# Latent attention in fp32 splits: staging of one group's rotary weights, and the queue of the output's first operands

## The chip, the cores and the metric

The kernel runs on one core of a Trainium2 chip. The metric is the device time of one execution in microseconds (us). Engines are named as in the profile: PE (TensorE), DVE (VectorE), ACT (ScalarE), POOL (GpSimd) and SP (SyncE, which only issues transfers here).

## The reference

One transformer layer on a sequence of S = 2048 rows of HID = 512: multi-head latent attention with 16 heads, residual and layer norm, then a linear layer with a scale and a bias, residual and layer norm.

```python
cq = rms_norm(x @ w_qa.T, q_a_ln_w)                  # 384 wide
q  = (cq @ w_qb.T)  -> 16 heads of 128 "nope" + 64 rotary
ckv = x @ w_kva.T                                    # 128 latent + 64 rotary
kv  = rms_norm(ckv[:, :128]) @ w_kvb.T               # k_nope 128, v 128 per head
scores = (q_nope . k_nope + rot(q_pe) . rot(k_pe)) * 192**-0.5   # causal
out = softmax(scores) @ v @ w_o.T
x = layernorm(x + out)
x = layernorm(x + (x @ (weight * scale_weight).T + bias))
```

## The kernel before

**The arithmetic.** Products in fp32 are made of two parts, a high one in the PE's fast fp32 format and the rest, so each product is three matmuls: high by high, high by low, low by high. The helper `split` makes both parts: ACT copies the high part (L64, or L67 with a scale) and DVE subtracts it (L65, L68). Keys are kept as latent rows: `Kn` (normalised latent, columns of keys) and `Kp` (rotary part), both for all 2048 keys, two parts each. Queries are brought into the latent space instead, by a weight product per head.

**Weights of the queries.** The heads come in four groups g of four. `weights_q(g)` prepares a group. For each of three slices `lt` it loads the rotary weights `rpe` (L159, on ACT's queue), splits them with the norm weight `qln` into a staging tile, and SP writes that to the DRAM tile `wpe_d[g]` (L169). Then for each slice it loads `wqb` (L174, ACT's queue), multiplies it on PE with `wk` (`ps_wq`, L179), splits the product into a staging tile and SP writes it to `wq_d[g]`. Both are loaded back when a pair of heads is projected: `wq` (`load_wq`, L352) and `wpe` (`load_wpe`, L358), by way of `move` (L59), on POOL's queue in block 0. Group 0 has a direct form: its split parts go to `wq0` and `wpe0` for the first use, and the second half of each product goes through staging tiles `wst` (L186).

**Staging.** `places` gives the staging tiles of groups 1 to 3. Keys beyond 1024 aren't used until later blocks, so 512-column pieces A to D of `Kn` and `Kp` (A and B are columns 1536 to 2047, C and D 1024 to 1535) serve as staging. Where `places` holds None, a tile of the ring with tag `st` is taken: three buffers, which `wst`, `cqst` (the compressed queries' staging) and group 1's `wpst` share. Raw loads share the tag `wraw`, with four buffers.

**Blocks and units.** The queries come in NB = 4 blocks of 512 rows, and in each block the heads come in eight pairs. Block 0 (128 to 512 keys) runs together with the projection of the rest of x and with the preparation of groups 1 to 3; there an automatic scheduler sets the order of the instructions on every engine. From block 1 on, PE and SP run in program order, and from the first pair's second quarter of block 3 ACT and DVE do as well (L729). POOL's place is always the scheduler's. In block 3 a unit is one head and one quarter of the rows, k = 0 to 7 in a pair:

- `head_scores`: PE makes the scores in two PSUM tiles (L438), DVE takes the maximum (L510), ACT the exponential into a tile `pr` (L532). Three PSUM tiles rotate, and the `pr` tiles have five buffers.
- `head_probs`: ACT makes a half-precision high part of `pr` (L563) and POOL the low part (L564), DVE transposes (L546), and SP writes the result into a `ring` in SBUF with four transfers (`turn`, L553). A `pr` tile is free again only when its ring transfers have landed.
- `values`: later, PE multiplies the ring's probabilities with V (L619). The result is scaled and goes to DRAM as `ot_d`.

**The output.** The output weights `wo` and the value weights `wv` are multiplied into `wvo` per pair (`value_output`, PE tile `ps_wo`, L198). `prepare_output(b, p, k)` runs ahead of each unit of the last block and loads what the output needs first: `wv` in pair 6 before unit 2, and in pair 7 `wo0` before unit 1, the attention results `o` with their inverse row sums `iv` of block 0, pair 0 and 1 (`latent_load`, L823, and `latent_rows`, L839), before units 2 and 3, and `wo1` before unit 4. `latent_split` uses `o` and `iv` before units 5 and 6 (L849). A third `o` is loaded before unit 7 on POOL's queue. `accumulate` (L888) adds the output's products.

```python
        if (p, k) == (NPAIR - 2, 2):
            state["wv"] = blk.tile([P, H, P], F32, tag="pe", name="wv")
            nc.gpsimd.dma_start(state["wv"], a["wv"])
```

## Time and profile before

| what | value |
|---|---|
| time, median of 3 runs | 1637.24 us (1637.19 to 1637.43) |
| the profiled execution: time, span | 1638.56 us, 1636.8 us |
| mean granted PE clock | 0.99 |
| busy share of the span: PE, DVE, ACT, POOL | 96%, 69%, 56%, 52% |
| longest ACT wait for a ring transfer; in all | 4.9 us; 61.1 us |
| PE idle for the exponential (L532) before scores | 13.9 us in 10 waits |

A line of the timeline has the start in us, the busy time in us, the engine, the source line, the operation with output and inputs, the shape and the count; in brackets stand the idle time of the engine ahead of it and what ended that. ACTq, POOLq and SPq are the same engines when they issue transfers. A window's line has the window, its length, and the busy time of PE, PE's weight loads, DVE, ACT and POOL with the number of instructions, then the mean granted PE clock, the mean busy share of the DMA engines and GB/s. The clock row shows the granted clock in tenths of full speed for 40 equal slices; 9 is 90% or more.

### The profile page before, as it was taken

The page shows a single profiled execution, that of the slowest core. Times are in us where ns is not written, and L with a number is a line of the kernel's source. Part 1 is how long each engine was busy: PE and PEld are TensorE (multiplying, and loading weights), DVE is VectorE, ACT ScalarE, POOL GpSimd, SP SyncE. Part 2 cuts the span into 40 slices and gives each one's busy share as a digit, 9 for nine tenths or more (in the row PEclk, how much of TensorE's full clock was granted, in tenths as well). Part 3 has the DMA queues.
Part 4 walks back from the last instruction along what each step waited for, and adds up shares of the span by engine and source line. Part 5 has one row for each costly group of instructions (what it writes and reads, how often), then busy time and mean ns, then how long its engine had stood idle before and what let it go on. Part 6 is the DMA issues. An engine that isn't in the chain of part 4 may idle for free. (4 is left out here: it accounts for less than half of the span.)

```text
span 1636.8 us, 27536 instructions
## 1 busy us (share of the span) xinstructions
PE 1575.2 (96%) x9292; PEld 1294.5 (79%) x9292; DVE 1130.0 (69%) x1874; ACT 918.3 (56%) x1529; POOL 846.0 (52%) x701
## 2 busy tenths in 40 slices
PE   9799998899999999999999999999999998999998
PEld 7688876788888888888887778888887776678876
DVE  5668665577677777777777678778677676575464
ACT  5557564666665757666665665666666654321120
POOL 2345553454554766667765566666666665011011
PEclk9899999999999999999999999999999999999999
DMA  6988676676776878787787767867777777962030
GB/s 213 265 238 267 194 203 164 175 185 172 191 206 171 217 179 202 162 206 181 199 195 180 177 153 174 184 160 160 177 156 192 211 178 210 320 197 77 32 117 33
DMA packets 259436, 297.60 MB, mean 182 GB/s; under 512 B 35264, under 2 KB 227136, under 8 KB 258272
## 3 DMA queue, kind: packets, MB, share of 16 engines
q1 hardware_dynamic: 241008, 251.63, 55.4%
q0 software_dynamic: 11376, 34.52, 12.0%
q10 hardware_dynamic: 6912, 9.70, 2.0%
q8 instruction: 74, 1.21, 0.3%
q14 instruction: 66, 0.54, 0.1%
HBM read 99.94 MB, written 36.44 MB: 83 GB/s over the span
## 5 line engine op out<-in xcount | busy, mean ns | idle before, releaser
L564 POOL TENSOR_TENSOR hlpr<-pr,hlpr 128x1024 f16<-128x1024 f32 (+3 forms) x320 | 613.2, 1935 | 327.2 <-ACT hlpr L563 297.9
L438 PE MATMUL s<-Kn,qn 128*128 128x512 f32 (+4 forms) x1920 | 510.3, 373 | 22.3 <-ACT pr L532 13.9
L532 ACT ACTIVATE pr<-s,bias,rq 128x1024 f32<-128x1024 f32 (+3 forms) x320 | 325.4, 1021 | 343.2 <-issue 178.3
L510 DVE TENSOR_REDUCE neg<-s 128x1 f32<-128x1024 f32 (+3 forms) x320 | 310.0, 985 | 133.2 <-PE s L441 75.0
L438 PEld LDWEIGHTS s<-Kn,qn 128*128 128x128 f32 x1920 | 334.3, 189 | 72.7 <-ACT pr L532 19.9
L619 PE MATMUL o<-ring,V 128*128 128x256 f16 x3024 | 373.1, 273 | 7.4 <-DMA ring<-pr 5.3
L546 DVE STREAM_TRANSPOSE pr<-hlpr 128x1024 f32<-128x1024 f32 (+7 forms) x256 | 311.5, 1223 | 97.9 <-POOL hlpr L564 72.2
L438 PE MATMUL s<-Kp,pe 128*128 128x512 f32 (+4 forms) x1280 | 362.9, 364 | 5.5 <-DMA pe<-prod 5.5
L619 PEld LDWEIGHTS <-V 128*128 128x128 f16 x3264 | 301.1, 96 | 82.7 <-issue 32.0
L563 ACT ACTIVATE hlpr<-pr 128x1024 f16<-128x1024 f32 (+3 forms) x320 | 338.2, 1113 | 4.9 <-DVE pr L546 1.0
L438 PEld LDWEIGHTS s<-Kp,pe 128*128 128x128 f32 x1280 | 233.6, 189 | 36.4 <-DMA pe<-prod 5.7
L410 PE MATMUL ps_qn<-cq,wq 128*128 128x512 f32 x576 | 150.0, 405 | 2.1 <-DMA wq<-wq_d 1.9
L989 POOL TENSOR_TENSOR lnr<-lnt,nhalf 128x1 f32<-128x1 f32 x32 | 21.3, 671 | 213.3 <-DVE lnt L988 213.2
L410 PEld LDWEIGHTS ps_qn<-cq,wq 128*128 128x128 f32 x576 | 105.5, 192 | 23.1 <-DVE xl L65 1.1
L68 DVE SCALAR_TENSOR_TENSOR qn<-ps_qn,kvln,qn 128x512 fp32r<-128x512 f32 x64 | 47.5, 744 | 45.5 <-ACT qn L67 45.2
L599 POOL TENSOR_TENSOR hl<-pr,hl 128x128 f16<-128x128 f32 (+3 forms) x64 | 56.8, 908 | 37.7 <-ACT hl L598 37.3
L372 PE MATMUL ps_pe<-cq,wpe 128*128 128x512 f32 x288 | 75.3, 407 | 0.2 <-DMA cq<-cq_d 0.2
L64 ACT ACTIVATE oh<-o 128x1024 fp32r<-128x1024 f32 x28 | 29.7, 1061 | 79.6 <-PE acc L888 49.1
L888 PE MATMUL acc<-wvo,oh 128*128 128x512 f32 x224 | 71.5, 401 | 1.0 <-ACT pr L532 0.6
L64 ACT ACTIVATE xt<-tp 128x512 fp32r<-128x512 f32 x16 | 9.6, 598 | 94.8 <-PE tp L1008 94.8
L532 ACT ACTIVATION_READ_ACCUMULATOR pr<-s,bias,rq 128x1 f32 x320 | 61.8, 193 | 0.0
L372 PEld LDWEIGHTS ps_pe<-cq,wpe 128*128 128x128 f32 x288 | 53.4, 193 | 10.6 <-issue 0.3
(458 smaller groups left out, 1777.4 us busy)
## 6 DMA issues: line engine op xcount, KB each, us to landing
ring<-pr SPq DMA_DIRECT2D x384, 128.0 KB, 2.9
wq<-wq_d SPq DMA_DIRECT2D x22, 768.0 KB, 6.7
ring<-pr SPq DMA_DIRECT2D x128, 112.0 KB, 3.4
o<-ot_d SPq DMA_DIRECT2D x28, 512.0 KB, 5.5
ot_d<-ot SPq DMA_DIRECT2D x97, 128.0 KB, 2.7
ring<-pr SPq DMA_DIRECT2D x128, 96.0 KB, 2.4
ring<-pr SPq DMA_DIRECT2D x64, 192.0 KB, 4.1
ring<-pr SPq DMA_DIRECT2D x64, 176.0 KB, 5.3
```

The lines of the kernel that those rows point to most:

```text
L68: nc.vector.scalar_tensor_tensor(l, ps, scale, h.bitcast(F32), ALU.mult, ALU.subtract)
L372: nc.tensor.matmul(ps, w[:, i, lt, x * P : (x + 1) * P], cq[:, k, lt, :], start=n == 0, stop=n == 8)
L410: nc.tensor.matmul(ps, w[:, i, lt, j * P : (j + 1) * P], cq[:, k, lt, :], start=n == 0, stop=n == 8)
L438: nc.tensor.matmul(ps[:, :w], lhs, K[:, i, c0 : c0 + w], start=n == 0, stop=n == 4 and not by_product)
L510: nc.vector.tensor_reduce(neg[:, ti : ti + 1], v, axis=AX.XY, op=ALU.max, negate=True)
L532: nc.scalar.activation(pr[:, x : x + n * w].rearrange("p (a c) -> p a c", a=n), v, AF.Exp, bias=bias, scale=r, accum_out=sums_of(b, p, qt, ...
L546: nc.vector.transpose(sq.rearrange("p (k c r) -> p k c r", k=4, r=32), words.rearrange("p (c k r) -> p k c r", k=4, r=32))
L563: nc.scalar.activation(hl[:, 0, c], pr[:, c], AF.Copy)
L564: nc.gpsimd.tensor_tensor(hl[:, 1, c], pr[:, c], hl[:, 0, c], ALU.subtract)
L599: nc.gpsimd.tensor_tensor(hl[:, j, 1, :], pr[:, j, :], hl[:, j, 0, :], ALU.subtract)
L619: nc.tensor.matmul(ps[:, :256], vt[:, i, k % 4, :], v[:, :, l, k, :], start=n == 0, stop=n == 3 * kts - 1)
L888: nc.tensor.matmul(acc, l[:, t, c], state["wvo"][p][:, i, j, :], start=p == 0 and j == 0 and n == 0, stop=p == NPAIR - 1 and j == 1 and n ...
```

## The change

Group 1's three rotary staging tiles come from the columns of keys and no longer from the ring `st`: two halves of A, and `Kn`'s columns 768 to 1023. Seven loads change their issuing queue from POOL's to ACT's: `wv`, `wo0`, `wo1`, and `o` and `iv` of pairs 0 and 1. ACT is one of the engines in program order there, and POOL isn't. `load_wo(2)` and `load_wo(3)` name SP's queue themselves and stay.

```diff
     places = [
-        [(None, None, None), (B, C, D)],
+        [(A[:, :, :256], A[:, :, 256:], Kn[:, :, 768:1024]), (B, C, D)],
         [(A[:, :, :256], A[:, :, 256:], None), (B, C, A)],
         [(A[:, :, :256], A[:, :, 256:], None), (B, A, B)],
     ]
...
-    def load_wo(g, pool, tag, by=nc.gpsimd.dma_start):
+    def load_wo(g, pool, tag, by=nc.scalar.dma_start):
...
         if (p, k) == (NPAIR - 2, 2):
             state["wv"] = blk.tile([P, H, P], F32, tag="pe", name="wv")
-            nc.gpsimd.dma_start(state["wv"], a["wv"])
+            nc.scalar.dma_start(state["wv"], a["wv"])
         if p == NPAIR - 1:
             if k == 1:
                 load_wo(0, blk, "qn")
             if k in (2, 3):
-                latent_load(0, k - 2, nc.gpsimd.dma_start)
+                latent_load(0, k - 2, nc.scalar.dma_start)
             if k == 4:
                 load_wo(1, state["pcr"], "wo")
```

## The prediction

> **What bounds the kernel now.** I read the page's engine shares first, then the clock row, then the busy time by windows, then the list of waits, and last the timelines of the two stretches that the change touches.

> ```profile
> PE 1575.2 (96%) x9292; PEld 1294.5 (79%) x9292; DVE 1130.0 (69%) x1874; ACT 918.3 (56%) x1529; POOL 846.0 (52%) x701
> ...
> PEclk9899999999999999999999999999999999999999
> ...
> 0.00:40.00 40.00, 35.98 (x216) 31.04 (x217) 22.80 (x57) 21.11 (x54) 11.27 (x32) 0.91 0.68 214
> 40.00:80.00 40.00, 30.09 (x184) 26.84 (x183) 24.82 (x50) 22.98 (x63) 14.21 (x23) 0.87 0.90 264
> 80.00:120.00 40.00, 40.00 (x274) 35.46 (x272) 25.97 (x54) 21.78 (x61) 18.84 (x34) 1.00 0.80 230
> ...
> 300.00:1240.00 940.00, 932.75 (x5703) 766.61 (x5702) 694.41 (x1111) 608.15 (x913) 588.02 (x385) 1.00 0.75 181
> ...
> 1280.00:1320.00 40.00, 36.03 (x222) 29.02 (x221) 25.57 (x39) 24.15 (x32) 27.48 (x21) 1.00 0.87 235
> ```

> TensorE (PE) is busy for 96% of the span, and from 300 to 1240 us it is busy for 932.75 of 940 us. A change that adds no matmul can gain only where PE stands still or runs slowly. The first column after the window's length is PE's busy time: PE lacks 9.9 us between 40 and 80 us, at a mean granted clock of 0.87, and 4.0 us between 1280 and 1320 us. Those are the places of the two edits.

> ```profile
> 35.91 0.51 ACT L67 ACTIVATE wpst<-rpe,qln 128x256 fp32r<-128x256 f32 x1 [4.21 <-DMA wq_d<-wst]
> ...
> 40.45 0.34 ACTq L174 DMA_DIRECT2D wqb<-in_wqb_dram  x1
> ...
> 46.05 2.05 PE L179 MATMUL ps_wq<-wk,wqb 128*128 128x128 f32 x8 [4.52 <-DMA wqb<-in_wqb_dram]
> ...
> 47.75 6.27 PE L410 MATMUL ps_qn<-cq,wq 128*128 128x512 f32 x18
> ...
> 49.77 0.56 POOL L59 DMA_DIRECT2D wpe<-wpe_d  x1 [10.57 <-DMA wpe_d<-wpst]
> ```

> This is the head. ScalarE (ACT) may split group 1's rotary weights only when the transfers that read group 0's `wst` out of the same ring of tiles have landed (4.21 us). The `wqb` load is issued after that on the same engine, and PE then waits 4.52 us for it. What follows on PE is slow as well.

> ```profile
> 1281.99 0.76 POOL L839 DMA_DIRECT2D iv<-inv_d  x1
> 1282.74 0.53 POOL L862 DMA_DIRECT2D wo<-in_wo_dram  x1
> ...
> 1293.16 1.10 ACT L532 ACTIVATE pr<-s,bias,rq 128x896 f32<-128x896 f32 x1 [4.86 <-DMA ring<-pr]
> ...
> 1295.69 4.43 POOL L564 TENSOR_TENSOR hlpr<-pr,hlpr 128x1024 f16<-128x1024 f32 x2 [7.12 <-ACT hlpr L563]
> ...
> 1299.35 0.97 PE L438 MATMUL s<-Kn,qn 128*128 128x512 f32 x3 [2.34 <-ACT pr L532]
> ...
> 1314.50 0.71 PE L438 MATMUL s<-Kn,qn 128*128 128x320 f32 x3 [1.63 <-ACT pr L532]
> ```

> This is pair 6 of the last block. GpSimd (POOL) issues two `o`, two `iv` and `wo0` in one bunch, 3 MB within 3.1 us, although they belong to pair 7. The ring transfers land late, ACT waits 4.86 us for them to free a `pr` tile, and PE waits for the exponentials. The chain of waits is transfer, ACT, PE.

> **Edit 1, the staging.** The same six ACT and VectorE (DVE) splits, three `wpe_d` writes and loads remain; only what they wait for changes.

> Removed: the 4.52 us wait for `wqb`, and the slow stretch behind it. The granted clock is 0.5 from 45.0 to 51.9 us. In it, the 18 matmuls of `ps_qn` take 6.27 us against 4.36 us for the same group at 30.60, and the 8 of `ps_wq` take 2.05 against 1.05 us at 40.36. That is 1.9 + 1.0 = 2.9 us, so at most 4.5 + 2.9 = 7.4 us.

> [...]

> Added: without the ring's wait, the compiled order puts the three splits far forward on ACT, between the `wqa_h` splits and the first `junk`, each with its DVE half. Their `rpe` loads are issued at 3.4, 7.9 and 8.3 us. L159 shows 5.8 us median to landing and 8.4 at most, so the second lands near 13.7 and the third near 16.2 us. ACT runs in order: the last two `wqa_h` pieces (10.9 in the trace), `junk` (11.76 and 12.75) and the `xh` splits (13.52) queue behind these waits, and PE waits for them. `junk` starts at about 16.7 in place of 12.75, the later `xh` at 17.2 in place of 13.5. PE, which had cover from `ps_cq` until about 18.0 us, then starts its next groups about 3.4 us later. I bound the loss at 2.4 us (some is caught up by 27 us, where PE had gaps of 0.85) and at 4.9 us (an `ACT` chain that lengthens); if these idle pieces also bring a slow stretch, 2.3 us more (half of 4.6 us of matmuls), so 7.2.

> Next late: the second pair's weights. POOL issues `wq<-wq_d` at 38.25 us; it needs all six `wq_d` writes, last issued at 33.6. They move back with the head, and the three `wpe_d` writes (768 KB) now run before them rather than after. With 2.4 to 4.9 us of delay, and 6.6 us to landing for this transfer, `wq` is there at 44.8 to 47.3 us, where the 18 `ps_qn` matmuls start at 47.75 in the trace. They then take 4.36 us and not 6.27. They end at 49.2 to 51.7 us against 54.0, a gain of 2.3 to 4.8 us, of which I take 3.5. From this I take off 1.0 us: the queries' rotary tile `pe` is issued from about 50 us, close to its use near 55 us, and the trace has no row for it being late there; the nearest is `pe<-prod` at 257.77, which cost 5.48 us. **Head: −2.5 us**, bounds −7.4 (nothing delayed) and +3 (delay of 7.2 against 4.5 regained).

> The other stalls of block 0 (13 us of PE between 240 and 300 us in the windows, 5.48 and 5.27 in single waits) move in time but not in kind, at 0 with ±2. From 80 to 240 us PE is busy enough that the time gained survives.

> **Edit 2, the queue.** Seven transfers leave POOL for ACT: `wv`, `wo0`, `wo1` of 1 MB each, and `o`, `iv` of pairs 0 and 1, 512 KB each. On ACT the order is fixed, so they follow the exponentials around them: `wv` near 1257 us, `wo0` 1316, the first `o` and `iv` 1320, the second near 1328, `wo1` near 1336.

> Removed: pair 6's stalls, 2.34 + 1.63 = 3.97 us on PE. By another measure, pair 6 takes 65.15 us and pair 5 58.20 for the same work, 7.0 us over; some of that is POOL's own issue time and waits of other causes, so I take 3.5. POOL loses seven issues of 0.53 to 0.77 us, 4.2 us together, on an engine that waits 7.12 us for ACT here.

> Added: seven issues on ACT, 0.33 to 0.6 us each, 3.2 us by an 0.46 mean; ACT is busy 24.15 of 40 us there, so most lies beside PE. The 4 MB of the last six come within 20 us around pair 7 rather than over 23 us in pair 6. And in the compiled programs the transfers of SP and ACT take turns on eight completion semaphores: the ring transfer that gets the semaphore last used by `wo0`, `o`, `iv` or `wo1` is issued only when that load has landed, and everything on SP waits behind it: the following ring transfers, and through them `pr`, ACT and PE. Landing of `wo` is 8.0 to 14.1 us after issue, of `wv` 8.5. Counting issue plus 8.5 against the ring transfer's own place, SP is held 0 to 3 us per load. The exponential at 1325.85 would start near 1328, 2.2 us late where PE has 0.7 us to spare: 1.5 us. The remaining three blocks cost 0 to 2 us; I take 0.5 for them together, nearest to the small waits of 0.55 and 1.06 that `wv` brought at 1256 and 1264. **Tail: −3.5 + 1.5 + 0.5 = −1.5 us**, bounds −7 and +5. `wo0` is needed at 1329.56, 13 us after its issue, inside its 8.0 to 14.1; `o` and `iv` at 1344.55, over 20 us after theirs.

> [...]

> **Sum.** −2.5 − 1.5 = −4.0 us. The profiled execution has a span of 1636.8 us and a time of 1638.56, 1.8 around it; less 4.0 it would be 1634.6. It lies 1.3 us above the median of 1637.24. On the median: **1633.2 us**.

> **Rivals.**
> Slower, by SP being held. If the ring transfers in pair 7 wait over 3 us for each load group (`wo0`; the first `o`, `iv`; the second; `wo1`), three of the four find no `pr` tile free and each costs PE a stall like the 2.34 us seen: 7.0 us, less pair 6's 3.5, with a head that gains nothing: +3.5, or 1640.7. Up to +5 with the head's bound. For: 0.87 of DMA time is in use already with the bunch in pair 6. Against: PE's work in pair 7 has value matmuls and `value_output` to fill with. It decides from 3 us of hold per load.

> No change: ACT's and DVE's early waits cost 3.4 us plus some slow clock, as much as the later stall gives back, and the bunch of loads costs pair 7 what it cost pair 6: 1637. For: at a head delay of 7.2 us, the upper bound, the wait for `wq<-wq_d` takes the whole place of the one for `wqb`.

> Full gain in both: the head's 7.4 us with the delay covered, and 4.0 us in the tail: 1637.2 − 11.4 = 1625.8. For: `ps_cq` matmuls cover part of ACT's wait. Against: in-order ACT.

> **How the numbers follow.** The forecast (−8 to −3.3 us, with the full gain in its outer part) has 0.52: 0.42 for the forecast, 0.10 for the full gain. No change has 0.20, slower by SP's hold or by a head beyond its +3 has 0.28. About 0.2%, 3.3 us, is what a measurement of this kernel tells from no change. The range takes in the full gain's 1625.8 and the slower rival's 1642.2: 1625.8 to 1642.2. The likeliest case by itself is 1629 to 1634.

> **What would show it.** Right: no wait for `wqb` near 46 us, `ps_qn` of 18 taking about 4.4 us, ACT waits for `rpe` near 11 to 16 us, PE a few microseconds late at 20 to 27 us; pair 6 near 60 us long. Wrong: a granted clock of 0.5 from 18 to 25 us; `wpe` or `pe` late around 55 us; ACT's waits for `ring<-pr` in pair 7 above those of pair 6; PE idle before `ps_wo`.

## The result, and the profile after

The changed kernel takes 1645.41 us, the median of 20 runs (1636.87 to 1657.98), beside 1637.22 us of the kernel before (20 runs). The ratio is 1.006, with an interval of 1.0046 to 1.0075: slower by 8.2 us between the medians and by some 9.8 us by the ratio, where 4 us faster was forecast. The profiled execution took 1645.51 us, with a span of 1643.7 us.

The runs of one kernel spread over 7 to 21 us, and some of that arises in block 0. The kernel e6 below has the order of before on PE up to 240 us, yet its trace, the slowest of its 12 runs, stands 8.4 us later than that of before at 167 us. So differences of 2 to 4 us between single traces are not used as a sum here; medians and ratios are.

The first fence is from the page of the profile of after, the second is its table by windows (length, busy time of PE, PE's loads, DVE, ACT and POOL, then clock, DMA share and GB/s).

```profile
PE 1580.6 (96%) x9292; PEld 1299.9 (79%) x9292; DVE 1131.1 (69%) x1874; ACT 917.2 (56%) x1529; POOL 841.7 (51%) x694
...
PEclk9999998999999999999999999999999999999999
```

```profile
0.00:40.00 40.00, 32.60 (x187) 27.06 (x188) 21.25 (x56) 20.45 (x55) 11.42 (x31) 0.96 0.74 236
40.00:80.00 40.00, 32.88 (x202) 28.81 (x200) 21.48 (x41) 19.38 (x52) 11.74 (x20) 0.91 0.70 226
...
240.00:280.00 40.00, 28.30 (x148) 22.78 (x148) 20.02 (x31) 15.35 (x33) 15.11 (x20) 0.83 0.56 141
...
1280.00:1320.00 40.00, 39.54 (x238) 32.50 (x237) 30.85 (x46) 27.37 (x36) 27.59 (x18) 1.00 0.72 155
1320.00:1360.00 40.00, 35.57 (x204) 27.23 (x203) 26.38 (x41) 20.99 (x28) 22.02 (x15) 0.91 0.86 233
```

Two windows of before that the prediction did not show:

```profile
240.00:280.00 40.00, 33.20 (x173) 27.18 (x171) 23.87 (x35) 17.30 (x30) 14.63 (x14) 0.91 0.59 155
...
1320.00:1360.00 40.00, 38.62 (x226) 30.14 (x225) 30.55 (x45) 24.83 (x33) 23.20 (x17) 1.00 0.68 158
```

The two edited places look much as intended: PE's busy time between 40 and 80 us rises from 30.09 to 32.88, and pair 6 (1280 to 1320) is nearly full at 39.54. What is paid is elsewhere: 3.4 us in the first 40 us, 3.1 us in pair 7, and 4.9 us between 240 and 280 us, where nothing was edited and the clock falls to 0.83. The windows go by time, and after runs up to 15 us late, so they don't hold quite the same work in both; the next table follows the work itself.

PE's place in the trace, by the start of the same `ps_qn` group in each kernel (difference to before, us):

| kernel | 94 us | 219 us | 304 us | 903 us | 965 us | span |
|---|---|---|---|---|---|---|
| after | +1.7 | +6.4 | +12.7 | +14.8 | +10.2 | +6.9 |
| staging alone (e1) | +2.3 | +5.8 | +10.8 | +12.4 | +7.5 | +3.3 |
| queue alone (e2) | +0.5 | +0.3 | +0.3 | +1.3 | +0.1 | −1.6 |
| after, `PT` ahead of `pe` (e9) | +2.5 | +6.3 | +3.3 | +3.4 | +1.8 | −2.4 |

In after and in e1 the largest step lies between 219 and 304 us: 6.3 and 5.0 us. The step ahead of it, from 94 to 219 us, is 4.7 and 3.5 us; e9 has it as well and ends level with before, and no run here explains it. This is the timeline from 219 us on, first of after, then of before; the number behind the start is the time that the issues took.

```profile
243.03 10.56 SPq L553 DMA_DIRECT2D PT<-pr  x15
254.09 1.84 SPq L393 DMA_DIRECT2D pe<-ph  x3
256.54 1.83 SPq L393 DMA_DIRECT2D pe<-prod  x3
258.42 1.00 SPq L393 DMA_DIRECT2D pe<-ph  x1
259.46 0.60 SPq L393 DMA_DIRECT2D pe<-prod  x1
260.11 1.47 SPq L553 DMA_DIRECT2D PT<-pr  x1
...
267.46 2.08 PE L619 MATMUL o<-PT,V 128*128 128x256 f16 x9 [11.44 <-DMA PT<-pr]
```

```profile
232.30 14.03 SPq L553 DMA_DIRECT2D PT<-pr  x20
246.43 0.74 SPq L478 DMA_DIRECT2D inv_d<-inv(0, 7)_3480  x1
247.50 1.86 SPq L393 DMA_DIRECT2D pe<-ph  x3
249.95 1.83 SPq L393 DMA_DIRECT2D pe<-prod  x3
...
257.77 0.90 PE L438 MATMUL s<-Kp,pe 128*128 128x320 f32 x2 [5.48 <-DMA pe<-prod]
```

In both kernels SP issues the probabilities of block 0's last pair (`PT`) and the eight transfers of block 1's first rotary queries (`pe`). In before all `PT` transfers come first. In after the scheduler has put the last `PT` transfer of the pair's third quarter behind the eight `pe` transfers: it goes out at 260.11 us instead of directly behind the fifteen, at 253.6. PE's order is the same in both kernels from 225 us on. PE needs that `PT` before anything that needs `pe`, and waits 11.44 us where it had waited 5.48. The granted clock is 0.5 from 259.8 to 273.5 us in after, 13.7 us long, and from 256.7 to 263.5 in before, 6.8 us.

The head of after:

```profile
13.97 0.51 ACT L67 ACTIVATE Kn<-rpe,qln 128x256 fp32r<-128x256 f32 x1 [3.36 <-DMA rpe<-in_wpe_dram]
...
50.15 5.96 PE L410 MATMUL ps_qn<-cq,wq 128*128 128x512 f32 x18 [2.20 <-DMA wq<-wq_d]
...
52.64 0.51 ACT L67 ACTIVATE Kn<-rpe,qln 128x256 fp32r<-128x256 f32 x1 [6.26 <-DMA rpe<-in_wpe_dram]
...
63.32 0.48 PE L438 MATMUL s<-Kp,pe 128*128 128x256 f32 x2 [2.90 <-DMA pe<-prod]
```

The wait for `wqb` is gone. ACT waits early for `rpe`, as foreseen, and `wq` is next late. Not foreseen is that group 2's `rpe` loads also move ahead, so that ACT waits 6.26 us for one at 52.64, and `pe` is late at 63.32.

### The profile page after: what moved, and what is told of

The parts are those of the page before. It is cut to its first block, busy times and chain, and to the rows that moved or that the text cites. A ratio compares the mean times of both kernels' runs of the same rounds, so it can differ in the third digit from the quotient of the medians.

```text
span 1643.7 us, 27524 instructions
## 1 busy us (share of the span) xinstructions
PE 1580.6 (96%) x9292; PEld 1299.9 (79%) x9292; DVE 1131.1 (69%) x1874; ACT 917.2 (56%) x1529; POOL 841.7 (51%) x694
## 3 DMA queue, kind: packets, MB, share of 16 engines
q0 software_dynamic: 10368, 29.27, 10.8%
## 5 line engine op out<-in xcount | busy, mean ns | idle before, releaser
L564 POOL TENSOR_TENSOR hlpr<-pr,hlpr 128x1024 f16<-128x1024 f32 (+3 forms) x320 | 612.3, 1932 | 328.9 <-ACT hlpr L563 306.7
L438 PE MATMUL s<-Kn,qn 128*128 128x512 f32 (+4 forms) x1920 | 512.5, 374 | 5.8 <-ACT pr L584 3.0
L532 ACT ACTIVATE pr<-s,bias,rq 128x1024 f32<-128x1024 f32 (+3 forms) x320 | 325.2, 1020 | 336.2 <-issue 184.0
L438 PEld LDWEIGHTS s<-Kn,qn 128*128 128x128 f32 x1920 | 336.9, 190 | 53.2 <-ACT pr L532 5.3
L438 PE MATMUL s<-Kp,pe 128*128 128x512 f32 (+4 forms) x1280 | 363.2, 364 | 2.9 <-DMA pe<-prod 2.9
L563 ACT ACTIVATE hlpr<-pr 128x1024 f16<-128x1024 f32 (+3 forms) x320 | 338.2, 1114 | 4.5 <-POOL hlpr L564 0.4
L438 PEld LDWEIGHTS s<-Kp,pe 128*128 128x128 f32 x1280 | 234.6, 190 | 34.0 <-DMA pe<-ph 3.1
L410 PE MATMUL ps_qn<-cq,wq 128*128 128x512 f32 x576 | 150.6, 407 | 5.9 <-DMA wq<-wq_d 5.5
L410 PEld LDWEIGHTS ps_qn<-cq,wq 128*128 128x128 f32 x576 | 105.6, 192 | 27.0 <-issue 6.1
L68 DVE SCALAR_TENSOR_TENSOR qn<-ps_qn,kvln,qn 128x512 fp32r<-128x512 f32 x64 | 47.6, 746 | 49.7 <-ACT qn L67 49.6
L532 ACT ACTIVATION_READ_ACCUMULATOR pr<-s,bias,rq 128x1 f32 x320 | 61.8, 193 | 0.0
```

Of the source, the lines that this page charges most:

```text
L68: nc.vector.scalar_tensor_tensor(l, ps, scale, h.bitcast(F32), ALU.mult, ALU.subtract)
L410: nc.tensor.matmul(ps, w[:, i, lt, j * P : (j + 1) * P], cq[:, k, lt, :], start=n == 0, stop=n == 8)
L438: nc.tensor.matmul(ps[:, :w], lhs, K[:, i, c0 : c0 + w], start=n == 0, stop=n == 4 and not by_product)
L532: nc.scalar.activation(pr[:, x : x + n * w].rearrange("p (a c) -> p a c", a=n), v, AF.Exp, bias=bias, scale=r, accum_out=sums_of(b, p, qt, ...
L563: nc.scalar.activation(hl[:, 0, c], pr[:, c], AF.Copy)
L564: nc.gpsimd.tensor_tensor(hl[:, 1, c], pr[:, c], hl[:, 0, c], ALU.subtract)
```

## The experiments

Each kernel was timed 10 to 12 times beside the kernel before, whose median was 1636.77 (e1 to e4), 1637.21 (e5 to e8) and 1638.64 us (e9 to e12). Read the ratios; 0.001 is 1.6 us. The changed kernel was not timed again beside them, so a comparison with it goes through the ratios to before, and the difference of two ratios is uncertain by some 3 to 4 us either way. All compute the whole layer.

**Each edit alone.** e1 keeps only the staging:

```diff
-        [(None, None, None), (B, C, D)],
+        [(A[:, :, :256], A[:, :, 256:], Kn[:, :, 768:1024]), (B, C, D)],
```

> Only the first edit (group 1's rotary tiles in columns of keys); the seven loads stay on POOL's queue. In the trace of the changed kernel PE is 2.4 us late at the second pair's ps_qn, 6.4 us late by 237 us, and 11.2 us late after a wait of 11.44 us for a PT transfer that SP issues behind eight pe transfers. Compiled with this edit alone, SP issues that PT transfer ahead of the pe transfers, as before the change. Theory A (the early ACT waits for rpe and the order of SP both cost): about 6 us slower than before, 1642 to 1645, with no PE wait above 8 us for PT. Theory B (the order of SP is nothing, the loss lies in the early waits and what follows): 11 us or more slower, 1648. Rival C (the queue edit is what costs): no difference from before, within 2 us.

Measured: 1643.37 us, ratio 1.0047 (1.0030 to 1.0064). The time is as expected, but by luck, since a premise was mistaken: the trace of e1 has the displaced `PT` as well, with a PE wait of 11.24 us at 266.85. The order of PE, ACT, DVE and SP is that of after. So e1 cannot tell early waits from the displaced transfer; it only says that the staging carries the loss.

e2 keeps only the seven loads on ACT's queue (one of them shown):

```diff
-            nc.gpsimd.dma_start(state["wv"], a["wv"])
+            nc.scalar.dma_start(state["wv"], a["wv"])
```

> Only the second edit (seven loads on ACT's queue); the staging is that of before, and PE, DVE and SP have the same order as before to the last instruction. Theory A (pair 6 gains the 5.9 us and pair 7 gives back the 5.7 us seen in the traces): within 1.5 us of before. Theory B (the prediction's tail): 1.5 to 3 us faster. Rival C (the whole loss is here): 6 us or more slower, with PE waits in pair 7 above 4 us and none of the head's changes.

Measured: 1636.66 us, ratio 0.9997 (0.9982 to 1.0011): no difference. It is not that nothing happened. From the `ps_qn` near 1276 us to the first `ps_wo`, pair 6's stretch, the trace of before takes 53.7 us and those of e2 and of after 49.0: 4.7 us gained. From the first to the fifth `ps_wo`, in pair 7, before takes 42.3 us and e2 47.8: 5.5 us given back. The timeline of e2 shows how:

```profile
1315.09 0.34 ACTq L823 DMA_DIRECT2D o<-ot_d  x1
1315.46 0.48 ACTq L839 DMA_DIRECT2D iv<-inv_d  x1
...
1321.68 0.54 SPq L553 DMA_DIRECT2D ring<-pr  x1
...
1324.24 0.54 SPq L553 DMA_DIRECT2D ring<-pr  x1
...
1333.73 0.99 ACT L532 ACTIVATE pr<-s,bias,rq 128x768 f32<-128x768 f32 x1 [4.66 <-DMA ring<-pr]
...
1336.23 2.07 PE L198 MATMUL ps_wo<-wo,wv 128*128 128x512 f32 x2 [4.41 <-DVE pad L468]
```

The `o` issued at 1315.09 takes 6.6 us to land, the `iv` at 1315.46 takes 8.8: they land at 1321.66 and 1324.23, and SP goes on at 1321.68 and 1324.24. (The last section has the same pairs in after, with their semaphores.) These two holds cost SP 1.4 and 2.0 us; `wo1` holds it for 1.7 us at 1339.76 and `wo0` for 0.4 at 1313.57. The second `o` and `iv` hold it for nothing: a wait of 1.9 us at 1332.44 was ended by one of SP's own ring transfers. ACT's longest waits for the ring move from pair 6 to pair 7, and PE waits 4.41 us there, for DVE.

e5 asks whether the place of the loads alone does it. The loads stay on POOL's queue, and POOL runs in program order from pair 6 of the last block:

```diff
+                if (b, p, qt) == (NB - 1, NPAIR - 2, 0):
+                    ctx_f.enter_context(tc.manual_schedule(engines={ET.PE, ET.SP, ET.DVE, ET.Activation, ET.Pool}))
```

> Before, with POOL too in program order from pair 6 of the last block on; the seven loads stay on POOL's queue, but now leave at the same places of the program as on ACT's queue, on POOL's own semaphores. Theory A (in the second edit, SP's ring transfers are held until o, iv and wo1 have landed, because they share semaphores with ACT's loads): pair 6 gains about 5.9 us as there, pair 7 gives back 2.5 us or less, no hold of SP above 1 us when a load lands; 2 to 4 us faster than before. Theory B (the bytes themselves crowd the transfer engines in pair 7): pair 7 gives back as much as with ACT's queue, within 1.5 us of before. Rival C (POOL's other work suffers in program order): 2 us slower or more.

Measured: 1642.54 us, ratio 1.0033 (1.0012 to 1.0053): slower. In its trace the fifth `ps_wo` starts at 1371.83, as in before (1371.88), and 5.0 us are lost behind it, in the output layers. There the order on PE, ACT and DVE differs from that of before as well, so that POOL's other work is what suffers is likely, not shown. Pair 6 became full (40.00 of 40 us) and pair 7 fell to 34.93 of 40. By the stretches used for e2, pair 6 takes 49.7 us (4.0 gained) and pair 7 45.6 (3.3 given back), with none of these loads on ACT's queue and no wait of SP that the trace puts down to one of them. So part of what pair 7 gives back comes with the place of the loads alone; but other work of POOL was reordered too, and how much of pair 7 is SP's hold and how much the transfers' load stays open.

**The order on SP.** Two added `yield`s put the rest of block 1's first projection, with the `pe` transfers, later in the program. e3 is after with them, e6 is before with them:

```diff
         split(rp, ph, pl)
+        if (b, g) == (1, 0):
+            yield
+            yield
         pe = blk.tile([P, 4, QB], F32R, tag="pe", name=f"pe{b}_{g}")
```

> Both edits, and the transfers of the first pe tile of block 1 are put two steps later in the program, so that SP issues all four PT transfers of block 0's last pair, third quarter, ahead of them. Theory A (that displaced PT transfer costs about 5 us of the loss): 1640 to 1641, some 5 us faster than the changed kernel, PE's wait for PT of 11.44 us gone, in its place a wait of at most 6 us for pe. Theory B (the stall at that place comes from the backlog of transfers, whatever their order): no faster than the changed kernel, 1644 to 1647, the wait of 10 us or more stays under another name.

> Before, with the transfers of block 1's first pe tile two steps later in the program; the compiled order of SP stays as it was around them. A control for the run of both edits with the same step. Theory A (that run's gain of 5 us came from the displaced PT transfer): within 1.5 us of before, 1635.5 to 1638. Theory B (the later step is a gain by itself): 4 us faster or more.

Measured: e3 1640.54 us, ratio 1.0028 (1.0013 to 1.0043); e6 1631.05 us, ratio 0.9965 (0.9952 to 0.9977). So by the medians e3 gains 4.9 us on after, but the step is a gain of 6.2 us on before as well, which has no displaced transfer. e6 is faster than both kernels. SP's order in it is that of before throughout, but PE takes more value matmuls of block 0 (`o<-PT`) ahead of block 1's `ps_qn`, and its wait of 5.48 us for `pe` becomes 1.46 at 263.31. Of the stretches in the table, its trace is 1.7 us shorter than before from 219 to 304 us, but 4.8 us shorter from 903 to 965, shortly behind a place where DVE's order is another too. So the step does more than restore an order, and e3 does not show what the displaced transfer costs.

e9 is the clean test. In after, the `PT` transfers of two quarters get precedence. The order of PE, ACT, DVE and POOL stays that of after; SP alone changes, where `PT7_2`, that of the last pair's third quarter, is ahead of the eight `pe` transfers again and a few `PT` transfers swap places:

```diff
-        turn(PT[:, : 4 * nk], 0, words, pr.rearrange("p j n -> p (j n)"))
+        if (p, qt) in ((7, 1), (7, 2)):
+            with tc.high_priority():
+                turn(PT[:, : 4 * nk], 0, words, pr.rearrange("p j n -> p (j n)"))
+        else:
+            turn(PT[:, : 4 * nk], 0, words, pr.rearrange("p j n -> p (j n)"))
```

> Both edits; the PT transfers of block 0's last pair, second and third quarter, are given priority, so that SP issues all of them ahead of the eight pe transfers. PE, ACT, DVE and POOL keep the order of the changed kernel to the last instruction. In the traces, the stretch from 222 to 304 us takes 90.2 to 91.5 us in the three kernels with one PT transfer behind the pe transfers and 85.2 to 85.7 us in the three with the order of before. Theory A (that order of SP is worth these 5 us): 1640 to 1641.5. Theory B (what costs is the backlog of transfers itself; the order only names the wait): 1644 to 1647.

Measured: 1637.87 us, ratio 0.9995 (0.9974 to 1.0016). The ratio is 0.0065 below that of after, some 10.6 us (7.5 us between the medians): the whole loss is gone, more than was expected. Its timeline:

```profile
242.93 10.78 SPq L553 DMA_DIRECT2D PT<-pr  x16
253.82 2.15 SPq L393 DMA_DIRECT2D pe<-ph  x2
...
257.34 0.80 PE L623 MATMUL o<-PT,V 128*128 128x256 f16 x3 [4.91 <-DMA PT<-pr]
```

Sixteen `PT` transfers stand ahead of `pe` in place of fifteen, and PE's wait of 11.44 us is one of 4.91. From the `ps_qn` near 219 us to the one near 304 us, e9 takes 82.3 us, after 91.5, e1 90.2, before and e2 85.2.

All the traces fall in with this. The four with a displaced `PT` (e4 and e10 below are the others) take 90.2 to 91.5 us, the three with SP's order of before 85.2 to 85.7, and e9, e3, e7, e11 and e12 82.3 to 82.7; only e6 (83.5) and e8 (85.2) lie apart. So the displaced transfer costs 5 to 6 us against before, and in e9 this stretch is some 3 us shorter even than in before. e9 takes the whole loss away, but does not show that all of it arose here. `inv_d` stays behind `pe` in e9, at 260.05, so its place is not what costs.

**The head.** e4 changes before in the other way: group 1's `wqb` loop goes ahead of its rotary loop, and the ring is kept. e7 is e4 with `pe` later, e8 is e7 with the new staging.

```diff
-        for lt in range(LT):
...
+        def rotary():
+            for lt in range(LT):
...
+        if g != 1:
+            rotary()
         for lt in range(LT):
...
+        if g == 1:
+            rotary()
```

> Before, with group 1's products (the wqb loads and ps_wq) put ahead of its rotary weights in the program; the rotary weights keep the ring of staging tiles. ACT then loads wqb before it waits for the ring, and has no wait for rpe early on. The compiled order has the displaced PT transfer as in the changed kernel. Theory A (the 4.52 us wait for wqb and its slow clock can be had without the early waits, and the displaced transfer costs 5 us): PE no wait for wqb, ps_qn of the second pair about 3 to 5 us earlier than before, then a long wait for PT near 260 us; sum within 3 us of before. Theory B (the head's loss in the changed kernel comes from the wait for wq that replaces the one for wqb, whatever ACT does): the second pair's ps_qn no earlier than before; with the displaced transfer 5 us slower.

> The run with group 1's products ahead of its rotary weights, staging as before, and the pe transfers two steps later, so that no PT transfer is displaced. Theory A (the displaced transfer costs about 4 us there too): about 1635, 2 us faster than before, and PE's wait of 9.24 us for PT is at most 5 us. Theory B (order is not it): 1638 to 1640, as without the step.

> The first edit's staging, with group 1's products ahead of its rotary weights, and the pe transfers two steps later; the seven loads on POOL as before. The rotary splits then stand behind the first junk and xh splits on ACT, with no early wait for rpe. Theory A (what is left of the first edit's loss, some 4 us, comes from ACT waiting for rpe in the first 16 us): PE's start of the second pair's ps_qn 3 us earlier than in the changed kernel or more, and 1635 to 1637. Theory B (it comes from the order that staging in the key columns brings later in block 0, at 150 to 215 us): 1640, whatever happens in the first 50 us.

Measured: e4 1638.94 us, ratio 1.0015 (0.9998 to 1.0032); e7 1632.53, 0.9976 (0.9963 to 0.9989); e8 1635.67, 0.9994 (0.9980 to 1.0007). In e4 the second `ps_qn` group starts at 43.17 us, 4.6 us earlier than in before; at 95 us PE is 0.9 us later. A gain at the head did not live to 95 us. e4 also has a displaced `PT` (9.24 us of wait), by another edit; with `pe` later (e7) 6.4 us come back. The new staging on top (e8) costs 3.1 us by the medians, at the edge of what the intervals tell apart.

The last three take the early waits away from after: group 1's `rpe` loads go on SP's queue. e10 does that alone, e11 together with the step of e9, e12 together with the two `yield`s.

```diff
-                nc.scalar.dma_start(raw, a["wpe"][:, lt, g])
+                (nc.sync if g == 1 else nc.scalar).dma_start(raw, a["wpe"][:, lt, g])
```

> Both edits; only group 1's three rpe loads move from ACT's queue to SP's, behind the other first loads. ACT's splits of them then stand behind the junk, xh and first cq splits; the displaced PT transfer is as in the changed kernel. The order of DVE at the start of block 3 is that of before, with a 128x1536 transpose between the two bias steps, which took 3.3 us more in the traces (59.3 to 62.2 us for four kernels against 57.2 to 58.5 us for six). Theory A (ACT's early waits for rpe and what they put off cost 5 to 8 us): 1641 to 1644, that is 5 to 8 less and 3.3 more than 1645.4. Theory B (the early waits cost nothing in the end): 1647 to 1650.

> Both edits, group 1's rpe loads on SP's queue and the PT transfers ahead of the pe transfers. The order of DVE at the start of block 3 has the transpose between the bias steps, as before the change. Theory A (early waits and displaced transfer together are the loss): 1636 to 1639, that is before within 2 us, since the staging by itself is worth nothing. Theory B (staging in the key columns costs by itself): 1641 or more. Rival C (without its two side effects the staging gains what was hoped for): 1634 or less.

> Both edits, group 1's rpe loads on SP's queue, and the transfers of block 1's first pe tile two steps later, as in the run of both edits with that step (1640.5). Both have the favourable order of DVE at the start of block 3, so the difference is that of the early waits alone. Theory A (early waits cost 5 to 8 us): 1632 to 1636. Theory B (they cost nothing in the end): 1639 to 1642.

Measured: e10 1641.86 us, ratio 1.0022 (1.0003 to 1.0041); e11 1638.55, 1.0000 (0.9982 to 1.0019); e12 1636.88, 0.9990 (0.9971 to 1.0009). In e10 the three splits start between 18.26 and 19.31 us without a wait for `rpe`, and PE still waits 11.57 us for `PT` at 266.00. Without the early waits the ratio falls by 0.0038 (after to e10, e3 to e12), some 6 us; the time of e12 lies between its two theories. But where `PT` goes first, their removal brings nothing (e9 to e11: 0.9995 to 1.0000). With both cures the staging is worth nothing either way.

The terms do not add. By the ratios `PT` first takes away 10.6 us, the absence of early waits about 6, both together 9.8. The intervals leave room for some 6 to 15 us for the first and 2 to 10 for the second. What stays open is why the early waits cost nothing once the transfer is in place.

## Why the prediction was wrong

**The step that failed** is the sentence on "the other stalls of block 0", which were to "move in time but not in kind, at 0 with ±2". The edit changed the automatic scheduler's order on SP some 200 us behind the edited code: one `PT` transfer went behind eight `pe` transfers. In place of 0 with ±2, the stretch from 219 to 304 us measured 6.3 us longer in after and 5.0 in e1, and e9 shows that putting the transfer back is enough to be rid of the loss. The prediction followed the reordering on ACT in the head and never asked the same of SP at the end of block 0, though it had singled out the stall of 5.48 us there by itself. (PE lacks 12.1 us between 240 and 300 us by the windows, not 13.) A compiled order can be read before any run, but the reading has to be right: the expectation for e1 had it the other way round from the trace.

**Head, −2.5 us.** The chain was right in its parts: no wait for `wqb`, early waits for `rpe` (3.36 us measured), PE late by 5.5 us at its first `ps_qn` (36.10 against 30.60), `wq` next late. The size was wrong at the last step: `wq` came at 50.15 us, not at 44.8 to 47.3. Most of that is a slip in the sum: 38.25 and a delay of 2.4 to 4.9 and 6.6 to landing make 47.3 to 49.8, so the gain of 2.3 to 4.8 us should have read −0.1 to 2.4. The rest is size: POOL issued `wq` at 43.93 us, 5.7 later than before, and the 18 matmuls took 5.96 us, not 4.36. They end at 56.1 us against 54.0, so +2.1 in place of −3.5. The `pe` tile's late arrival, taken at 1.0 us, was 2.90. Time gained did not live long either: in e4 the 4.6 us gained at 43 us were all but gone by 80. And the sentence that from 80 to 240 us "the time gained survives" is doubtful: the traces of e10 and e11 stand 2.5 and 2.7 us ahead of before at 94 us, and 4.7 and 2.5 us behind it at 219.

A shorter wait than the 4.52 us of before went with a slow stretch here: in after the 18 `ps_qn` matmuls behind the wait of 2.20 us took 5.96 us, with a granted clock of 0.5 from 51.6 to 55.0, while in e9 the same group behind a wait of 1.73 us took 4.34. What goes with it is told in the last section. The head's own slow stretch, one of the prediction's signs of being wrong, came true: the granted clock is 0.5 from 20.9 to 24.3 us in after. Even so its mean over the first 40 us was higher than before, 0.96 against 0.91.

**Tail, −1.5 us.** e2 gives −0.5 us with about 2.4 to either side, so the sum is not contradicted, but both terms were too small: −4.7 for −3.5 in pair 6, and +5.5 for +2.0 in pair 7. The mechanism of the hold was as described: in e2 SP went on 0.02 and 0.01 us behind the landings. Per load group it was 0.4 us (`wo0`), 3.4 (the first `o` and `iv`), nothing (the second) and 1.7 (`wo1`), so one group of four passed the 3 us from which the rival was to decide; yet the price in pair 7 came nearer to that rival's 7.0 than to 2.0. The prediction's marker, "ACT's waits for `ring<-pr` in pair 7 above those of pair 6", came true, and so did PE idle before `ps_wo` (4.41 us in e2).

**The rivals.** Slower came true, but by neither of the ways named: SP's hold was paid for by pair 6, and at 95 us the head was only 1.7 us late. No case held the reordering on SP at the end of block 0.

## What to carry to other kernels

Where a scheduler sets an order, an edit is priced on every queue to the end of the scheduled stretch, not around the edited lines: compare the compiled orders, and look first at the queues whose stalls the profile already shows. The one transfer here that was needed first and issued behind eight others went out 6.5 us late, and PE's wait grew by 6.0 us; the time at half clock went from 6.8 to 13.7 us with it. Gains in a stretch where the DMA engines are as busy as here in the first 95 us (a DMA share of 0.7 to 0.9; e4's 4.6 us gained at 43 us were a loss of 0.9 at 95) are to be taken at nothing until a later landmark shows them.

## What was not expected of the hardware

Transfers issued by two engines were tied to each other to within 0.1 us: in e2, SP went on at 1321.68 and 1324.24 us, when ACT's `o` and `iv` landed at 1321.66 and 1324.23. In the traces of before and after, the transfers of SP and ACT name the same eight semaphores (100, 102, 111 and 114 to 118), those of POOL eight others (103 to 110). In after, ACT's `wo0` (111), first `o` (114) and first `iv` (115) landed at 1324.06, 1332.36 and 1334.80 us, and the ring transfers that wait for 111, 114 and 115 went out at 1324.08, 1332.37 and 1334.82.

At the start of block 3 a stall of 2.31 us was followed by a slow stretch in before, with a granted clock of 0.5 from 949.56 to 952.97 us:

```profile
948.14 0.72 PE L438 MATMUL s<-Kn,qn 128*128 128x320 f32 x3 [2.31 <-ACT pr L532]
...
949.98 3.95 PE L619 MATMUL o<-ring,V 128*128 128x256 f16 x21
```

Another 21 value matmuls of this shape take 2.49 us at 941.01. In after this stall is 0.46 us, and the stretch between the `ps_qn` groups near 903 and 965 us takes 57.6 us against 62.2: the change gets 4.6 us back there, far behind the edited lines. DVE's order differs between the two shortly ahead of this place (up to 892 us in before). That the order is the cause is not shown: e9 has the order of after on DVE and took 60.5 us with a stall of 1.88. No kernel changed this place by itself.
